# Side work around the first sum of a chunk, in a kernel of four selective-scan layers

## The chip, the cores and the metric

The kernel runs on one core of one Trainium2 chip. The metric is the device time of one execution in microseconds (us); lower is better. TensorE is called PE in the profile (its weight loads PEld), VectorE DVE, ScalarE ACT, GpSimd POOL, and SyncE, which issues the DMAs, SP.

## The reference

Four layers of a vision Mamba block run one after the other over `x` of shape 8 x 48 x 48 x 96, each as `x = x + layer(groupnorm(x))`. A layer projects 96 channels to 2 x 192 (`xz`), puts one half through a depthwise 3x3 convolution and SiLU (`u`), and scans it in four directions: by rows and by columns, forward and backward. Layers 0 to 2 compute this, at each of the 2304 places of a direction, with a state of 16 values per channel:

```python
dA = jnp.exp(dl[..., None] * A)
h = h * dA + (dl * u)[..., None] * Bv[:, :, None, :]
y = jnp.einsum('bkdn,bkn->bkd', h, Cv)
```

`dl` is the softplus of a low-rank projection of `u`; `Bv` and `Cv` are projections of `u`. The four directions are added up with a skip term, normalised over channels, multiplied by `silu(z)` (the other half of `xz`) and projected back to 96 channels. Layer 3 has the same frame with another form of the scan.

## The kernel before

**Tiles and units.** Two images make a pair, four pairs a layer. The 192 channels of a pair lie in three tiles of 128 partitions: 128 channels of either image (t = 0, 1) and the last 64 of both (t = 2). A tile, a phase (ph, rows or columns) and a direction (d) make a group, twelve per pair. The 2304 places of a group are cut into three chunks of 768, and a chunk takes 16 units, one for each n of the 16 states. So a pair has 36 chunks and 576 units. The twelve pairs of layers 0 to 2 have 6912 units; layer 3 ("short") is done in another way, on the places near the ends alone (class `Edge`), and is not touched by the change.

**One unit.** For its n, ACT computes dA (`exp`, L726), TensorE spreads row B over the partitions in PSUM (`spread`, L743), VectorE multiplies it by du = dl * u (L755) and scans (L759), GpSimd multiplies the states by C (L768), and TensorE adds the product to the sum `acc` (`add_up`, L804). In every fourth unit (n % 4 == 3, `pooled`) B comes from a DMA and is multiplied by GpSimd (L698); VectorE then only scans, and dA is put into PSUM instead of B, in `get_ready` of the unit before.

**The sum.** `acc` lies in two banks of PSUM, in a pool with one buffer. `add_up(0)` of a chunk opens it (L798: a matmul of u with the skip weights, or of y so far with the identity), then adds. `add_up(15)` closes it and puts `collect` on the list `late_sums`; `collect` (L819) is ACT's copy of the sum into y. A chunk that is the last of a forward group (`turns`) is not copied: the first chunk of the backward group covers the same places and adds to the same sum, without opening. So a pair has 36 ends of chunks, 30 with a copy and 6 where the sum goes on.

**The order of the work.** `run` writes the order out by hand, unit after unit, and `keep_order` ties every instruction to the one before it on its engine. A unit k issues, in this order: the copy of a sum that the unit before closed (`collected()`, which returns whether there was one: `busy`), what the next units need (`get_ready(k + 1)`: loads three units ahead, the spread of unit k + 1, the decay of unit k + 3), the carries of the scan before (`catch_up`, L650), its own scan, the sum of unit k - 4 (`LAG` = 4), one step of `coming` and one side step. With the lag of four, the last sum of a chunk falls into the unit with n = 3 of the next chunk, and the copy and the next opening into the unit with n = 4. Below these are called unit 3 and unit 4, and so for other n.

**Three kinds of work go on beside.** All are generators of which a step is taken by `next`.
- `coming` is `prepare` of the next chunk: it makes dl and du in two halves (ACT L590 to L601, GpSimd L603 and L604, VectorE L607 to L614), one step per unit from n = 0 on. Between the step of GpSimd and that of L607 stand two bare `yield`s in a row.
- `ahead` is the `prologue` of the next pair: group norm, input projection, convolution (L301, two matmuls of the profile for each of nine taps and five pieces), the x-projection (L454) and its DMAs. `rest` is what is left of the first pair's own prologue.
- `behind` is the `epilogue` of the pair before: for each of 16 pieces of three rows the layer norm, the gate `silu(z)` (L259, with an activation table load ahead of it and one, L260, after it), the product with it (VectorE, L1031) and the output projection, in twelve steps.

`side_step` takes one step of `rest`, or else of `behind` or `ahead`: first the one that holds a PSUM bank (it yielded True), then the one that has made the smaller share of its estimated steps. A prologue whose next tile has no room yet yields `GATED` and gives way. At n = 0 of the last chunk of a pair what is left of both is done at once (`drain`).

Of the kernel before, what the change touches and what calls it, by code (L numbers as in the profile page):

```python
# [53 lines left out]
NS = 16  # L54
# [48 lines left out]
def ss2d_layers_kernel(ctx: ExitStack, tc: tile.TileContext, x_in, consts, weights, out):  # L103
# [449 lines left out]
    def load_dt(c):  # L553
        r = layers[c.l].rank
        c.dts = sm2.tile([64, SCAN], F32, name="dts", tag="dts")
        for b in c.batches:
            q0 = 32 * b if c.t == 2 else 0
            nc.sync.dma_start(
                c.dts[q0 : q0 + r, : c.m],
                state[c.l, c.p]["xd"][c.ph, b, c.d * r : (c.d + 1) * r, c.c0 : c.c0 + c.m],  # L560
            )
# [80 lines left out]
    def collected():  # L642
        some = bool(late_sums)
        while late_sums:
            late_sums.pop(0)()
        return some

    def catch_up():
        while late_act:
            nc.scalar.copy(*late_act.pop(0))  # L650
# [421 lines left out]
    def drain(g):  # L1072
        for _ in g:
            pass

    def step(g):
        next(g, None)
# [7 lines left out]
    def side_step(*sides):  # L1085

        for s in sorted(sides, key=lambda s: (not s.held, s.made / s.total)):
            got = next(s.g, s)
            s.held = got is True
            if got is not s and got is not GATED:  # L1090
                s.made += 1
                return True
        return False
# [3 lines left out]
    def mark():  # L1097
        marks.append(len(tc._region_blocks()[0].instructions))
# [12 lines left out]
    LAG = 4  # L1111
    LOADS, DECAYS = 3, 2

    def run(pairs, short):


        def units():
            for l, p in pairs:
                for gi, (t, ph, d) in enumerate(groups):
                    if l in short:  # L1120
                        c = Edge(l, p, t, ph, d)
                        for i in range(NS // QUAD):
                            yield (l, p, gi * (NS // QUAD) + i), c, i
                        continue
                    group = {}
                    for i in range(len(SCANS)):
                        c = Chunk(l, p, t, ph, d, i, group, c if d == 1 and i == 0 else None)
                        for n in range(NS):
                            yield (l, p, (gi * len(SCANS) + i) * NS + n), c, n

        def begin(l, p, first=False):
            if l not in layers:
                layers[l] = Layer(l)
            return prologue(l, p, l in short, first)

        todo = list(units())

        def get_ready(k):

            def early(ahead, what):  # L1140
                for i in range(0 if k == 0 else k + ahead, min(k + ahead + 1, len(todo))):
                    getattr(todo[i][1], what)(todo[i][2])

            early(LOADS + 1, "load_b")
            early(LOADS, "load")
            if k == 0:
                todo[0][1].decay(todo[0][2])
            if k < len(todo):
                (l, p, _), c, n = todo[k]
                if n == 0 and c.first and l not in short:  # L1150
                    c.group["carry"] = capool.tile([P, NS], F32, name="carry", tag="carry")
                c.spread(n)
            early(DECAYS, "weigh")
            for i in range(k + DECAYS if k else 1, min(k + DECAYS + 1, len(todo))):
                todo[i][1].decay(todo[i][2])

        rest = begin(*pairs[0], first=True)
        while next(rest) is not READY:
            pass
        rest = Side(rest)  # L1160
        chunks = list(dict.fromkeys(c for _, c, _ in todo))
        drain(prepare(chunks[0]))
        behind = ahead = Side()
        coming = iter(())
        done = None
        mark()
        get_ready(0)
        for k, ((l, p, unit), c, n) in enumerate(todo):
            at = pairs.index((l, p))
            following = pairs[at + 1] if at + 1 < len(pairs) else None  # L1170
            if l in short and unit == 0:
                mark()
            per = NS // QUAD if l in short else NS
            all_units = len(groups) * (per if l in short else len(SCANS) * per)
            place["tiles"] = 3 * unit // all_units
            if done:
                behind, done = Side(epilogue(*done), 195), None
            if unit == LAG and following:
                ahead = Side(begin(*following), 300)
            if n == 0:  # L1180
                drain(coming)
                if unit + per == all_units:
                    drain(behind.g)
                    drain(ahead.g)
                coming_to = chunks.index(c) + 1
                coming = prepare(chunks[coming_to]) if coming_to < len(chunks) else iter(())
            if n == max(0, per - 1 - DECAYS):
                drain(coming)
            if n == 10 and coming_to + 1 < len(chunks):
                z = chunks[coming_to + 1]  # L1190
                if (z.l, z.p) == (l, p):
                    load_dt(z)
            busy = collected()
            get_ready(k + 1)
            catch_up()
            c.scan(n)
            if k >= LAG:
                (bl, bp, _), b, bn = todo[k - LAG]
                b.add_up(bn)
                if todo[k - LAG + 1][0][:2] != (bl, bp):  # L1200
                    done = bl, bp
            step(coming)

            for _ in range(10 if l in short else 0 if busy else 1):
                side_step(rest) or side_step(behind, ahead)
        for _, c, n in todo[-LAG:]:
            collected()
            c.add_up(n)
            catch_up()
        collected()  # L1210
        drain(epilogue(*pairs[-1]))

    last = NLAYER - 1
    run([(l, p) for l in range(NLAYER) for p in range(NPAIR)], (last,))

    keep_order(*marks[:2])
# [8 lines left out]
    with tc.If(nc.values_load(again, min_val=0, max_val=1) > 0):  # L1225
        run([(last, p) for p in range(NPAIR)], ())
# [95 lines left out]
```

## Time and profile before

| what | value |
|---|---|
| median of 3 runs | 21,290.81 us (21,287.53 to 21,323.55) |
| the profiled execution, own time | 21,306.41 us |
| its span | 21,304.6 us |
| granted TensorE clock, mean | 0.944 |
| layers 0 to 2: last scan ends at | 19,386 us |
| DVE busy up to there | 17,933.5 us |
| DVE scan with a carry (L759), mean | 1,813 ns |
| DVE multiply (L755), mean | 947 ns |
| POOL product with C (L768), mean | 1,813 ns |
| ACT copy of a sum (L819), 360 times, mean | 1,131 ns |
| PE opening (L798), 4 matmuls of 751 (y) or 582 ns (u), mean | up to 3.0 us |
| PE sum (L804), 27,648 matmuls, four per unit, mean | 519 ns |
| ACT table load (L259, L260), 304 each | 1,283 ns |
| ACT SiLU of the epilogue (L259), mean | 515 ns |
| ACT SiLU over a whole u (L259), 48 times, mean | 2,124 ns |

A line of the timeline reads: start, duration, engine, source line, operation, tile written <- tiles read, form, count, and in brackets the engine's idle time just before it and what ended it. A line of the list of waits reads: engine and line that waited <- engine and line that ended the wait: microseconds in total, times, longest. The view of one source line lists who ended the idle time before its instructions, with microseconds and times.

### The profile page before, as it was taken

To read this page: it belongs to the slowest core of one execution; us is meant where nothing else is said; L and a number is where in the kernel's file an instruction comes from. 1 tells how busy PE (TensorE), PEld (TensorE's weight loads), DVE (VectorE), ACT (ScalarE), POOL (GpSimd) and SP (SyncE) were. 2 spreads that over 40 slices of the span, in tenths; PEclk is the share of its full clock that TensorE was granted. 3 is DMA by queue.
4 is the path that set the end of the run, shared out by engine and by line. 5 is a ranking of instruction groups with operands and counts; after the bars stand their busy time and mean duration, and the time that the engine had idled before them with its cause. 6 is when DMAs were issued, how large, how long until landed. Compare 5 with 4: busy or idle time off the path is not lost. (4 is left out here: it accounts for less than half of the span.)

```text
span 21304.6 us, 229326 instructions
## 1 busy us (share of the span) xinstructions
PE 18651.1 (88%) x64610; PEld 9183.5 (43%) x64610; DVE 18839.5 (88%) x15938; ACT 13518.2 (63%) x23969; POOL 17988.3 (84%) x11081
## 2 busy tenths in 40 slices
PE   8988988998998998998998988988988988988886
PEld 3333443443443443443443443443443443444555
DVE  6999999999999999999999999999999999997453
ACT  5655666666666665665665666665665665666776
POOL 5989898888899899899898889889889888896442
PEclk8999999999999999999999999999999999999887
DMA  4666676676676676676676666666666666664221
GB/s 136 195 190 192 190 196 192 188 192 193 190 198 195 187 200 193 187 202 196 187 200 192 191 193 195 186 194 194 186 195 192 187 194 191 189 193 124 78 72 52
DMA packets 1707633, 3832.97 MB, mean 180 GB/s; under 512 B 238448, under 2 KB 575216, under 8 KB 1693168
## 3 DMA queue, kind: packets, MB, share of 16 engines
q1 hardware_dynamic: 1706352, 3818.21, 61.5%
q8 instruction: 521, 8.54, 0.2%
q14 instruction: 760, 6.23, 0.1%
HBM read 3665.08 MB, written 152.27 MB: 179 GB/s over the span
## 5 line engine op out<-in xcount | busy, mean ns | idle before, releaser
L804 PE MATMUL acc<-cb,cst 128*128 128x384 f32 x27648 | 10772.4, 519 | 0.0
L768 POOL TENSOR_TENSOR cb<-cb,da 128x768 f32<-128x768 f32 x5184 | 9350.0, 1813 | 1586.3 <-DVE da L759 953.8
L804 PEld LDWEIGHTS acc<-cb,cst 128*128 128x128 f32 x27648 | 5031.9, 197 | 3972.4 <-issue 1530.2
L759 DVE TENSOR_TENSOR_SCAN da<-da,carry,b 128x768 f32<-128x768 f32 x3456 | 6267.3, 1813 | 219.0 <-DVE b L755 1.4
L755 DVE TENSOR_TENSOR b<-du,b 128x768 f32<-128x768 f32 x5184 | 4910.0, 947 | 789.6 <-PE b L743 780.1
L726 ACT ACTIVATE da<-dl,a 128x768 f32<-128x768 f32 x5184 | 4770.6, 926 | 94.0 <-POOL cb L768 61.2
L743 PE MATMUL b<-brow,pick 48*128 48x512 bf16 (+3 forms) x10368 | 2660.3, 338 | 1516.2 <-DVE da L759 1184.7
L726 ACT ACTIVATE b<-dl,a 128x768 f32<-128x768 f32 x1728 | 1560.5, 903 | 2927.1 <-DVE da L759 2673.6
L768 POOL TENSOR_TENSOR cb<-cb,bb 128x768 f32<-128x768 f32 x1728 | 3133.2, 1813 | 188.1 <-issue 63.6
L698 POOL TENSOR_TENSOR bb<-bb,du 128x768 f32<-128x768 f32 x1728 | 3131.4, 1812 | 124.5 <-DMA bb<-xd 78.8
L759 DVE TENSOR_TENSOR_SCAN da<-da,b 128x768 f32<-128x768 f32 x1728 | 3029.5, 1753 | 107.4 <-DVE b L755 0.9
L743 PEld LDWEIGHTS <-pick 48*128 48x128 bf16 (+1 forms) x10368 | 667.2, 97 | 4345.3 <-DVE da L759 2285.7
L759 DVE TENSOR_TENSOR_SCAN bb<-b,carry,bb 128x768 f32<-128x768 f32 x1152 | 2069.7, 1797 | 9.1 <-ACT b L726 6.1
L301 PE MATMUL ps<-pad,diag 128*128 128x480 f32 (+1 forms) x4320 | 1995.8, 560 | 17.0 <-DVE du L611 11.5
L650 ACT COPY carry<-da 128x1 f32<-128x1 f32 x3456 | 626.9, 181 | 1068.6 <-DVE da L759 1055.7
L590 ACT ACTIVATE ps<-ps,w 128x384 f32<-128x384 f32 (+1 forms) x912 | 496.6, 545 | 1115.0 <-PE ps L585 1114.4
L301 PEld LDWEIGHTS ps<-pad,diag 128*128 128x128 f32 x4320 | 807.4, 192 | 721.1 <-issue 293.4
L603 POOL TENSOR_TENSOR lg<-lg,w 128x384 f32<-128x384 f32 (+1 forms) x912 | 891.5, 977 | 196.7 <-ACT w L601 196.6
L759 DVE TENSOR_TENSOR_SCAN bb<-b,bb 128x768 f32<-128x768 f32 x576 | 999.2, 1735 | 15.5 <-ACT b L726 11.9
L585 PE MATMUL ps<-dts,w 6*128 6x384 f32 (+5 forms) x2432 | 819.7, 522 | 182.0 <-DVE du L611 65.9
L604 POOL TENSOR_TENSOR lg<-lg,e 128x384 f32<-128x384 f32 (+1 forms) x912 | 889.3, 975 | 71.2
L798 PE MATMUL acc<-y,cst 128*128 128x384 f32 x1008 | 625.3, 751 | 275.2 <-ACT y L819 176.2
(141 smaller groups left out, 17322.1 us busy)
## 6 DMA issues: line engine op xcount, KB each, us to landing
cb<-xd SPq DMA_DIRECT2D x4736, 384.0 KB
cb<-xd SPq DMA_DIRECT2D x4736, 192.0 KB
bb<-xd SPq DMA_DIRECT2D x1152, 384.0 KB
bb<-xd SPq DMA_DIRECT2D x1152, 192.0 KB
yd<-y SPq DMA_DIRECT2D x48, 1152.0 KB
ey<-yd SPq DMA_DIRECT2D x256, 216.0 KB
brow<-xb SPq DMA_DIRECT2D x576, 72.0 KB
ex<-xs SPq DMA_DIRECT2D x256, 108.0 KB
```

Source lines behind the costliest of these rows:

```text
L301: nc.tensor.matmul(ps[:, :m], ly.diag[:, int(t == 2), j, :], pad[:, r0 + dy : r0 + dy + nr, dx : dx + W], start=(j == 0), stop=(j == 8),)
L585: nc.tensor.matmul(o[:, :m], ly.dtw[q0 : q0 + r, k, chans], dts[q0 : q0 + r, at], start=True, stop=True,)
L603: nc.gpsimd.tensor_sub(lg, lg, w1)
L604: nc.gpsimd.tensor_add(lg, lg, e)
L650: nc.scalar.copy(*late_act.pop(0))
L698: nc.gpsimd.tensor_mul(b, b, self.du)
L726: nc.scalar.activation(da, self.dl, AF.Exp, scale=columns_of(self.l, self.t, self.ph, self.d, n))
L743: nc.tensor.matmul(b[:, z : z + zm], w, self.brow[:k, z : z + zm], start=True, stop=True)
L755: nc.vector.tensor_mul(b, self.du, b)
L759: nc.vector.tensor_tensor_scan(way(h), way(da), way(b), start, ALU.mult, ALU.add)
L768: nc.gpsimd.tensor_mul(c, c, h)
L804: nc.tensor.matmul(self.acc[:, a, : self.m // 2], ident, c[:, a, :], start=False, stop=(n == NS - 1 and not self.turns),)
```

## The change

The step of `coming` and the side steps become a function, `beside`. In a unit in which a sum was copied (`busy`, unit 4) it is called ahead of `add_up`, with one side step where there was none; in every other unit it stays behind `add_up`. The unit whose `add_up` is the last of a chunk (`ends`, unit 3) has no side step any more, also where the sum goes on and nothing is copied; there, unit 4 keeps the side step that it had. So a pair has 540 side steps where it had 546. Layer 3 stays as it was.

```diff
             get_ready(k + 1)
             catch_up()
             c.scan(n)
+
+
+            def beside():
+                step(coming)
+
+                for _ in range(10 if l in short else 0 if ends else 1):
+                    side_step(rest) or side_step(behind, ahead)
+
+            ends = l not in short and k >= LAG and todo[k - LAG][2] == NS - 1
+            if busy and l not in short:
+                beside()
             if k >= LAG:
                 (bl, bp, _), b, bn = todo[k - LAG]
                 b.add_up(bn)
                 if todo[k - LAG + 1][0][:2] != (bl, bp):
                     done = bl, bp
-            step(coming)
-
-            for _ in range(10 if l in short else 0 if busy else 1):
-                side_step(rest) or side_step(behind, ahead)
+            if not (busy and l not in short):
+                beside()
```

## The prediction

> **What bounds the kernel now.** First the busy line, then one engine's idle time, then who ended it. The busy line of the page:
>
> ```profile
> PE 18651.1 (88%) x64610; PEld 9183.5 (43%) x64610; DVE 18839.5 (88%) x15938; ACT 13518.2 (63%) x23969; POOL 17988.3 (84%) x11081
> ```
>
> Three engines stand near 88%, so the average names no bound. By stretches, layers 0 to 2 end at 19,386 us, and there DVE is busy 17,933.5 us: it sets the pace, one scan of some 1.75 us per unit and a multiply of 0.95 us in three of four. Its idle time there is 1,453 us, and only that can be won. The list of waits and, second, the view of line 1031 up to 19,400 us, say what most of it waits for:
>
> ```profile
> DVE b L755 <- PE b L743: 780.1, 644, 4.8
> ...
> PEld acc L798 <- ACT y L819: 304.0, 187, 5.4
> ...
> PE acc L798 <- ACT y L819: 231.8, 149, 5.0
> ...
> ACT y L819 <- PE acc L804: 160.3, 172, 2.0
> ```
>
> ```profile
>   ACT ps L259: 73.5, 41
> ```
>
> L755 waits for its spread B (L743), TensorE waits at the opening sum (L798) for ACT's copy of the old one (L819), and the copy waits for the last sum in only 172 of 360 cases: in the others ACT itself came late. Counting L759's scans in program order (6912, 16 per chunk) gives every instruction its unit. The idle time then gathers: 410 us lie before the multiply of unit 6 at 359 chunk boundaries with a copy, 1,142 ns each (zero in the 72 boundaries whose sums go on), and 73 us before L1031, behind the scan of unit 3. One boundary in the timeline:
>
> ```profile
> 5267.11 1.73 DVE L759 TENSOR_TENSOR_SCAN bb<-b,bb 128x768 f32<-128x768 f32 x1
> ...
> 5267.68 1.56 PE L804 MATMUL acc<-cb,cst 128*128 128x384 f32 x4
> 5268.05 1.28 ACT L259 ACT_TABLE_LOAD   x1
> ...
> 5269.34 0.52 ACT L259 ACTIVATE ps<-ps 128x432 f32<-128x432 f32 x1
> 5269.87 1.28 ACT L260 ACT_TABLE_LOAD   x1
> 5269.89 0.60 DVE L1031 TENSOR_TENSOR eyc<-eyc,ps 128x432 f32<-128x432 f32 x1 [1.05 <-ACT ps L259]
> ...
> 5272.09 0.79 ACT L819 COPY y<-acc 128x768 f32<-128x768 f32 x1
> ...
> 5272.93 2.85 PE L798 MATMUL acc<-y,cst 128*128 128x384 f32 x4 [3.27 <-ACT y L819]
> ...
> 5277.94 0.96 DVE L755 TENSOR_TENSOR b<-du,b 128x768 f32<-128x768 f32 x1 [1.68 <-PE b L743]
> ```
>
> The last sum of the old chunk ends at 5269.2, but ACT is in a gated SiLU of the epilogue issued as side work of unit 2 (3.1 us with its two table loads); the copy starts 2.9 us late, TensorE stands 3.27 us, and the spread of unit 6, behind opening and first sum in TensorE's queue, is 1.68 us late for DVE. L1031, side work of unit 3, makes DVE wait for the same SiLU.
>
> **What the Trainium skill says.** "PSUM — Partial Sum Buffer", section "Engine vs sequencer instructions": the queues of ScalarE, VectorE and GpSimdE are strictly first in, first out, and matmuls start and end in program order. The trace agrees: no matmul passes the waiting L798. The same page, section "PSUM bank collisions raise a hardware error", wants accesses to a bank kept apart by semaphores; the trace has TensorE idle 535.8 us at L798 until L819 is done. "ScalarE: Activation LUTs", section "What ACT_TABLE_LOAD costs", states 1283 ns for the load and about 1380 ns of drain. The trace has the 1283 ns, but next to no gap: 5268.05 + 1.28 is 5269.33, and the activation starts at 5269.34. I take 1.28 + 0.52 + 1.28 = 3.08 us per SiLU.
>
> **The change, part by part.** The opening sum stands in unit 4 of a chunk, the last sum of the one before in unit 3.
>
> 1. *step(coming) ahead of the opening sum: 0.* In unit 4 it is the fifth step of prepare, which lies between two bare yields and issues nothing.
>
> 2. *The side step of unit 3 moves to unit 4, ahead of the opening sum.* On TensorE the order was last sum, side, spread 5, opening; it becomes last sum, spread 5, side, opening: the same sum of times before the opening, no gain. On ACT the step's work no longer stands ahead of the copy. It was there in 72 boundaries; taking it out of the traced order (the copy then starts at the later of the last sum's end and the ACT work before the side step) brings the copies forward by 37 us in all. Not all of it reaches DVE: 210 of 359 boundaries have a late unit 6. I take half: -18 us.
>
> 3. *What falls into units 1 and 2 shifts.* Where sums go on (72 boundaries) the side step of unit 3 is dropped, none is given back; all later side work of the pair slips by one step each time, six per pair. I walked the yields of prologue and epilogue through the loop's rules, before and after; for before, this puts a convolution into unit 3 111 times, as the trace has it. The sides come in a rhythm that met the boundaries badly: the epilogue's SiLU (192 in these layers) is the side step of unit 2 at 39 of the 359 boundaries, and of 13 with the new rule. At the 39, unit 6's wait is 2,514 ns, at the other 320, 975 ns: 26 x 1.54 = 40 us. The SiLU in unit 1 rises from 22 to 25, Ln and Exp (L1006) there from 8 to 14; such boundaries lie about 0.55 us above others of their kind: +5 us. Together -35 us.
>
> 4. *L1031 leaves unit 3.* DVE's wait for the SiLU, 73 us, ends there in every case, as nothing is issued in unit 3; the multiply then stands behind the scan of unit 4. In the 13 that keep their SiLU in unit 2, the copy is as late as before, and what is won at L1031 is lost in unit 6. The other 26 of 39 win: -49 us.
>
> 5. *Matmuls ahead of the opening.* The steps that now fall there hold 0.91 us of TensorE work per boundary, those of unit 3 held 0.77 (from rows such as L301's 576 ns, two per step): 0.14 x 359 = 51 us. TensorE idles before the opening at 263 of 359 (1,089 ns on average), which hides some of it; without that cover all 51 us would be exposed. A gain is excluded, as it is only more work on the same queue. I take 20.
>
> 6. *DMAs, POOL, DVE.* The step's DMAs pass the loads of unit 8 on SP's queue. Loads go out three units ahead (over 8 us), so 0. One is special: at a pair's start the epilogue's first load waits for the store of y (ey issued at 5014.66, 3.34 us after ex). It is now queued a unit earlier, and the loads for unit 9 wait behind it: at 11 changes of pair, 0 to 2 us each; the cover is three units; I take 0 and keep 22 as the end. POOL's side work (pad memsets, L434) slips by a unit; with 20 us at most in either direction, since POOL was idle over 3,300 us, I take 0. Slots: 540 per pair for some 495 to 520 steps; none is left for the drains, so 0.
>
> Sum: -18 - 35 - 49 + 20 = -82 us, that is about -80. The profiled execution took 21,306.4 us (span 21,304.6), so 21,226; it lies 16 us above the median of the three runs, and against that I say 21,211.
>
> **The rivals.**
> - *Nothing to be measured (0.22).* Other long ACT steps (the SiLU over a whole u, 4.7 us, comes into unit 2 at 6 boundaries) take the SiLU's place, and half of parts 3 and 4 is lost: -18 - 42 + 40 = -20, or 21,271. For: both are averages over few boundaries. Against: ACT side work ahead of the copy falls from 1.23 to 0.88 us per boundary in units 1 to 3.
> - *The copy was most of it (0.15).* The copy starts 748 ns after the last sum on average, 269 us in all. If the lighter units 1 to 3 end half of that, and the 73 us at L1031 go wholly: 135 + 73 - 20 (part 5) = 188: 21,103. Against: exps of L726 and prepare's steps lie in the same queue.
> - *Slower: side matmuls expose the opening (0.08).* Where the copy is done before TensorE has gone through the moved step, every matmul of it delays opening, first sum and spread 6, then DVE. It decides once the opening's idle time is used up: unit 6 is already late in 210 cases. Were all 51 us of part 5 exposed, the 22 of part 6 come in, and parts 3 and 4 only changed places with new bad meetings, -18 + 51 + 22 = +55: 21,346.
> - *That the change does not act* is excluded: the order on TensorE's queue is written out and kept.
>
> **How the numbers follow.** Forecast 0.55: 21,211, between 21,160 (part 5 hidden, part 2 whole) and 21,255 (part 5 exposed, the re-meeting half as good). The range takes in most of the larger gain and of the rival of no change: 21,100 to 21,290; what is left out is the slower case and the tails, under 0.2. About 0.2% (43 us) is what a measurement of this kernel can tell: faster means under 21,248. Nearly all of the forecast and all of the larger gain: 0.70; same 0.22; slower 0.08.
>
> **What would show it.** Right: L1031's wait for L259 before 19,400 us falls from 73.5 to almost nothing; L798's idle time until L819 falls from 535.8 to some 400; L755's for L743 from 780 to some 700; DVE's idle time in layers 0 to 2 loses 80 of 1,453 us, its busy time nothing. Wrong: L798 waits for something other than L819 or ACT's carries (the moved step waits itself), L1031's wait reappears in another unit, or the multiplies of units 8 and 9 take up what unit 6 gives back.

## The result and the profile after

| | before | changed |
|---|---|---|
| median of 4 runs | 21,290.11 us | 21,138.65 us |
| lowest to highest | 21,287.53 to 21,323.55 us | 21,131.57 to 21,152.58 us |
| ratio, 95% interval | | 0.9929 (0.9917 to 0.994) |
| profiled span | 21,304.6 us | 21,129.7 us |
| granted TensorE clock, mean | 0.944 | 0.951 |

The change gains 151 us, 0.71%, where 80 us had been forecast: the direction and the places were right, the size was nearly double. The busy line of the page after:

```profile
PE 18566.6 (88%) x64610; PEld 9118.1 (43%) x64610; DVE 18834.4 (89%) x15938; ACT 13520.6 (64%) x23969; POOL 17984.5 (85%) x11081
```

The instruction counts are those of before, and up to the last scan DVE is busy as long (17,933.5 us before, 17,926.9 now): only its idle time can have gone. TensorE is busy 85 us less with the same matmuls (18,651.1 before), and its granted clock is higher; what that has to do with the change is taken up with the second experiment. The lines of the list of waits that answer to those of before:

```profile
DVE b L755 <- PE b L743: 678.8, 619, 6.2
...
PEld acc L798 <- ACT y L819: 241.7, 248, 4.1
...
ACT y L819 <- PE acc L804: 177.4, 177, 4.1
...
PE acc L798 <- ACT y L819: 142.6, 139, 3.7
```

DVE waits 101 us less for its spread. The two lines of L798 behind L819 are the weight loads and the matmuls of the same openings, so most of one wait stands in both. Their sum, 535.8 us before and 384.3 now, which the prediction took for TensorE's idle time, counts it about twice. The matmul line alone falls by 89 us (231.8 to 142.6). Counted once per opening, whatever ended the wait, TensorE's idle time there falls from 391 to 258 us. The view of L1031 up to the last scan has nothing under "its engine sat idle before it" any more, where it had 73.5 us behind L259.

Counted by unit as in the prediction, the balance of layers 0 to 2 is: DVE's idle time from 1,452.5 to 1,294.1 us (-158), the last scan from 19,386.2 to 19,221.2 us. Of the 158, the multiply of unit 6 gives 105 (412.8 to 307.4), L1031 gives 74, L611 13; L607, the step of prepare that waits for GpSimd, takes 32 back.

### The profile page after: what moved, and what is told of

It is laid out like the page before. It is cut to its first block, busy times and chain, and to the rows that moved or that the text cites. A ratio compares the mean times of both kernels' runs of the same rounds, so it can differ in the third digit from the quotient of the medians.

```text
span 21129.7 us, 229163 instructions
## 1 busy us (share of the span) xinstructions
PE 18566.6 (88%) x64610; PEld 9118.1 (43%) x64610; DVE 18834.4 (89%) x15938; ACT 13520.6 (64%) x23969; POOL 17984.5 (85%) x11081
## 5 line engine op out<-in xcount | busy, mean ns | idle before, releaser
L755 DVE TENSOR_TENSOR b<-du,b 128x768 f32<-128x768 f32 x5184 | 4912.0, 948 | 685.4 <-PE b L743 678.8
L698 POOL TENSOR_TENSOR bb<-bb,du 128x768 f32<-128x768 f32 x1728 | 3131.3, 1812 | 183.4 <-DMA bb<-xd 142.8
L650 ACT COPY carry<-da 128x1 f32<-128x1 f32 x3456 | 627.1, 181 | 1086.3 <-DVE da L759 1076.4
L798 PE MATMUL acc<-y,cst 128*128 128x384 f32 x1008 | 619.1, 745 | 192.2 <-ACT y L819 127.2
```

What stands on the lines that cost most here:

```text
L698: nc.gpsimd.tensor_mul(b, b, self.du)
L755: nc.vector.tensor_mul(b, self.du, b)
```

## The experiments

All times are medians; the difference is against runs of the kernel before on the same chip, taken between them. The changed kernel stands at -151 us.

| run | us | against before | ratio, 95% interval |
|---|---|---|---|
| e1_move_only | 21,241.45 | -52 | 0.9973 (0.9963 to 0.9984) |
| e2_rhythm_only | 21,242.25 | -51 | 0.9976 (0.9966 to 0.9987) |
| e3_step_behind_sum | 21,361.29 | +68 | 1.0034 (1.0022 to 1.0046) |
| e4_spread_ahead | 21,088.52 | -205 | 0.9902 (0.9887 to 0.9917) |
| e8_before_no_silu | 21,107.37 | -185 | 0.9911 (0.9897 to 0.9924) |
| e5_after_no_silu | 21,175.85 | -117 | 0.9942 (0.9929 to 0.9956) |
| e6_both | 21,239.19 | -53 | 0.9974 (0.9965 to 0.9984) |
| e7_both_lighter | 20,910.43 | -382 | 0.9822 (0.9808 to 0.9835) |
| e9_spread_lighter | 20,926.78 | -362 | 0.9824 (0.981 to 0.9837) |
| e10_lighter_only | 21,169.55 | -119 | 0.9938 (0.9924 to 0.9951) |

**The move without the rhythm (e1_move_only).** To the changed kernel:

```diff
             ends = l not in short and k >= LAG and todo[k - LAG][2] == NS - 1
+            ends = busy and unit == LAG or ends and not todo[k - LAG][1].turns
```

> The side step moves from unit 3 to unit 4, ahead of the opening sum, but every step keeps its place in the rhythm: where the sum goes on, unit 3 keeps its step, and the epilogue starts in unit 5 as before, so the SiLU stays in unit 2 at 39 boundaries. By the prediction's terms (-18 for the copy, +20 for the matmuls, L1031's 73 us lost again in unit 6) it should stand within 20 us of the kernel before. The rival, that the move itself is most of the gain and was sized too small, expects -80 to -110 us. In both, L1031 waits for L259 no more.

It gains 52 us, which lies in neither of the expected ranges. Because every step keeps its place in the sequence, each boundary can be compared with itself, over the ten units from the scan of unit 1 to that of unit 10. At the 39 with the SiLU in unit 2, L1031's wait ends (73.5 to 0.4 us in the view of the line) and the wait of unit 6 grows from 2,514 to 3,854 ns; the ten units are 31 ns shorter. So what is won at L1031 is lost in unit 6, as forecast. At the 71 other boundaries whose moved step has ACT work, the copy starts 0.55 us nearer to the last sum, 39 us in all, and the ten units shrink by 680 ns (57 without matmuls) and 1,590 ns (14 with matmuls): 61 us in all. So more reaches DVE than the copies were moved by; the next experiment shows a reason. At the 189 where the step is matmuls alone it is 24 ns, 4.5 us in all: TensorE's order there is worth nothing, as forecast. The rest gives 17 us. (These sums come from the two profiled executions, whose spans differ by 81 us where the medians differ by 52; the shares are what counts.)

**The rhythm without the move (e2_rhythm_only).** To the kernel before:

```diff
-            for _ in range(10 if l in short else 0 if busy else 1):
+            ends = l not in short and k >= LAG and todo[k - LAG][2] == NS - 1
+            none = busy and unit != LAG or ends and todo[k - LAG][1].turns
+            for _ in range(10 if l in short else 0 if none else 1):
```

> The kernel before, with its side step still in unit 3 and none in unit 4, but with the rhythm of the changed kernel: no side step in unit 3 where the sum goes on, and the epilogue's first step in unit 4 of a pair. The SiLU then stands in unit 2 at 13 boundaries and not 39. The prediction's terms give -35 for the wait of unit 6 and -49 for L1031: about -84 us against before. The rival, that the move is most of it, expects -40 to -60 us here. L1031's wait for L259 should fall to a third, some 25 us.

It gains 51 us, not 84, as the rival said, and L1031's wait falls to 18.7 us. Move and rhythm alone give 52 + 51 = 103 us, together 151: there are some 48 us that neither has. The size is rough: each of the three figures has an interval of some 20 to 25 us either way, and the profiled spans give 20 us. The place is clear: at 16 boundaries the rhythm now puts a SiLU on the moved step itself. Against before, the ten units of these 16 lose 6 us by the move alone, gain 14 by the rhythm alone and gain 85 by both; at the other boundaries both together give 46 us less than their sum. Without the move this SiLU stands in unit 3, right ahead of the copy; the timeline of one of the 16, rhythm only:

```profile
7100.23 1.56 PE L804 MATMUL acc<-cb,cst 128*128 128x384 f32 x4
...
7102.53 1.28 ACT L259 ACT_TABLE_LOAD   x1
...
7103.83 0.52 ACT L259 ACTIVATE ps<-ps 128x432 f32<-128x432 f32 x1
...
7104.36 1.28 ACT L260 ACT_TABLE_LOAD   x1
...
7105.65 1.48 ACT L819 COPY y<-acc 128x768 f32<-128x768 f32 x1
...
7107.19 2.92 PE L798 MATMUL acc<-u,skip 128*128 128x384 f32 x4 [4.97 <-ACT carry L650]
...
7113.43 0.96 DVE L755 TENSOR_TENSOR b<-du,b 128x768 f32<-128x768 f32 x1 [5.71 <-PE b L743]
```

The same boundary in the changed kernel:

```profile
7081.78 1.56 PE L804 MATMUL acc<-cb,cst 128*128 128x384 f32 x4
...
7084.09 1.47 ACT L819 COPY y<-acc 128x768 f32<-128x768 f32 x1
...
7085.59 1.28 ACT L259 ACT_TABLE_LOAD   x1
...
7085.61 1.56 PE L798 MATMUL acc<-u,skip 128*128 128x384 f32 x4 [1.84 <-ACT carry L650]
...
7086.89 0.52 ACT L259 ACTIVATE ps<-ps 128x432 f32<-128x432 f32 x1
...
7087.42 1.28 ACT L260 ACT_TABLE_LOAD   x1
7088.22 0.54 DVE L607 SCALAR_TENSOR_TENSOR ps<-ps,lg 128x384 f32<-128x384 f32 x1
...
7088.39 0.50 PE L743 MATMUL b<-brow,pick 48*128 48x512 bf16 x2
...
7089.18 0.95 DVE L755 TENSOR_TENSOR b<-du,b 128x768 f32<-128x768 f32 x1
```

The SiLU's three ACT pieces are the same 3.1 us in both; ahead of the copy DVE waits 5.71 us at the multiply of unit 6, behind it not at all: the last line has no bracket. (The bracket of L798 names L650, a carry that ACT ran right behind the copy.)

The 5.71 us are more than the SiLU's 3.1. From the end of the last sum to the opening it is 5.40 us with the rhythm alone and 2.27 us in the changed kernel, which is the SiLU. From the opening to the multiply of unit 6 it is 6.24 and 3.57 us, though the same matmuls stand there (the opening takes 2.92 and 1.56 us). Below are these two stretches, first with the rhythm alone and then in the changed kernel; PEclk is the granted clock of TensorE as a share of full speed:

```profile
core 0: us, PE busy (x) PEld busy (x) DVE busy (x) ACT busy (x) POOL busy (x), PEclk, DMA share, GB/s
7107.19:7113.43 6.24, 6.24 (x11) 2.74 (x12) 0.53 (x3) 3.78 (x7) 3.61 (x3) 0.52 0.76 252
```

```profile
7085.61:7089.18 3.57, 3.57 (x11) 1.85 (x12) 3.47 (x4) 3.53 (x4) 3.49 (x4) 1.00 0.88 310
```

So about 3.1 us of the loss are the later copy, and about 2.7 us are the same matmuls taking longer at about half the clock. It is not this boundary alone. The clock records of these traces have two values, full and half. In the kernel before, the clock was half for some time between the opening and the multiply of unit 6 at 142 of the 359 boundaries, and 338 of the 410 us of unit 6's wait lie at these; in the changed kernel it was so at 74 boundaries, with 186 of 305 us. In the trace of before, half clock goes with a long idle time of TensorE just before the opening: it is there at 12 of 198 boundaries with less than 1 us, at 74 of 103 with 1 to 2 us, and at 56 of 58 with more. At the 71 boundaries of the first experiment the move takes the number of those with half clock from 39 to 18, which fits the 61 us won for 39 us of earlier copies. This suggests that the higher mean clock of the changed kernel comes, at least in part, from the shorter waits at the openings, and in turn shortens what follows them. No run sets the clock, so neither this nor the share of the whole gain that passes through it is shown.

Once more the table loads show no drain beside them, which "ScalarE: Activation LUTs" of the Trainium skill has in its section "What ACT_TABLE_LOAD costs": 7102.53 + 1.28 is 7103.81, and the SiLU starts at 7103.83. Over the 16 boundaries the wait of unit 6 is 79.5 us in this run and 8.1 us in the changed kernel, and their ten units 31.93 and 27.50 us: 16 x 4.43 = 71 us.

**The side step of unit 4 behind the sum (e3_step_behind_sum).** To the changed kernel:

```diff
-            if busy and l not in short:
-                beside()
             if k >= LAG:
...
-            if not (busy and l not in short):
-                beside()
+            beside()
```

> The changed kernel with the side step of unit 4 behind the opening and first sum, and none in unit 3. If the place ahead of the opening matters because the step's matmuls (0.91 us per boundary) use the time in which TensorE waits for the copy, they now stand between first sum and spread 6, and about 0.3 to 0.7 us comes back at the boundaries where unit 6 is late: +60 to +140 us against the changed kernel, so near -50 against before. If only ACT's order matters, it stays within 20 us of the changed kernel, at -150. In both, the start of the copy stays as in the changed kernel.

It is 219 us slower than the changed kernel and slower than before. Here the view of L798, the engine's idle time before it (again with loads and matmuls added up):

```profile
  ACT y L819: 634.5, 510
```

The copy starts 471 ns after the last sum on average (463 in the changed kernel), so ACT is not it. But TensorE now stands idle for the copy (1,199 ns per opening, 719 in the changed kernel) and runs the side step's matmuls later, between first sum and spread 6: the wait of unit 6 rises from 307 to 460 us. The boundaries with half clock between the opening and that multiply rise from 74 to 118. The direction was the first theory's, the size beyond its range (60 to 140 us).

**The spread of unit 6 ahead of the opening (e4_spread_ahead).** To the changed kernel:

```diff
-                c.spread(n)
+                if n not in c.b or c.pooled(n):
+                    c.spread(n)
...
             if busy and l not in short:
                 beside()
+                if l < NLAYER - 1:
+                    c.spread(n + 2)
```

> The changed kernel with the spread of unit 6 issued in unit 4 ahead of the opening, in layers 0 to 2. If the wait at unit 6 (305 us of DVE's idle time in the changed kernel) is only the spread's place behind opening and first sum, it goes; TensorE's queue is 0.5 us longer ahead of the opening and must first wait for the scan of unit 4, so the later units 8 and 9 take some of it back: -100 to -250 us against the changed kernel, -250 to -400 against before. The rival, that TensorE's backlog of opening and sums only moves on to the spread of unit 8, expects within 40 us of the changed kernel, with L755's wait in unit 8 or 9 grown by as much as unit 6 loses.

It beats the changed kernel by 54 us, which lies between the two expectations (100 us or more; 40 at most). The wait of unit 6 goes, from 307 to 3 us; that of unit 8 grows from 105 to 348. So most of it only moved on, which is the rival's mechanism, to the next spread behind the same matmuls: TensorE has a backlog.

**No SiLU near the copy (e8_before_no_silu, e5_after_no_silu).** A flag is up while a side's next step is a SiLU or the scaling of x (layer 3 is left as it is):

```diff
+            late = n in (1, 2, 3) and (place["long"] or place["gate"])
-            for _ in range(10 if l in short else 0 if busy else 1):
+            for _ in range(10 if l in short else 0 if busy or late else 1):
```

in the kernel before, and with `n in (1, 2)` in `beside` of the changed kernel.

> The kernel before, in which no side step is taken in units 1, 2 and 3 while the next one of a side would be a SiLU (or the group norm's scaling of x): such steps wait for unit 5 or later. Nothing else moves. If ACT work ahead of the copy is the cause, the wait at L1031 (73 us) goes and the wait of unit 6 falls from 412 to 300 us or less, and it gains 100 to 150 us against before, as much as the whole change, without any step moved ahead of the opening. The rival, that the place of the step ahead of the opening is what gains, expects no more than the 50 us of the rhythm alone.

> The changed kernel, with no side step in units 1 and 2 while the next one would be a SiLU or the scaling of x. By a walk through the rules 38 SiLUs of the epilogue and 7 over a whole u leave these units. If ACT's queue ahead of the copy is what is left to gain, -30 to -70 us against the changed kernel (-180 to -220 against before), the start of the copy is nearer to the last sum. If what is left at unit 6 is TensorE's own chain of opening and first sum, within 20 us of the changed kernel.

The first gains 185 us, more than the 100 to 150 expected and more than the whole change, and no side step in it is moved from unit 3 to unit 4: the wait of unit 6 falls from 413 to 254 us, L1031's from 74 to 7, and the boundaries with half clock behind the opening from 142 to 76. It is thus shown that taking ACT's long steps away from the copy is alone worth as much as the change. The second misses both expectations: the wait of unit 6 falls from 307 to 208 us, as the first theory wanted, but those of units 0, 1 and 8 rise by 81 us together and L607's by 17, and the run ends 35 us behind the changed kernel, with intervals that overlap. Postponed SiLUs gather in units 0 and 4 (28 and 32 by a walk through the rules, 12 and 16 before; the traces show the 32 and 16 of unit 4); that these cause the new waits is argued, not shown.

**Both, and a lighter backlog (e6_both, e7_both_lighter, e9_spread_lighter, e10_lighter_only).** e6 joins e4 and e5. The other three have, besides:

```diff
-                for _ in range(10 if l in short else 0 if ends else 1):
+                for _ in range(10 if l in short else 0 if ends or n in (5, 6) else 2 if n in (12, 13) else 1):
```

e7 has it (with `late`) on top of e6, e9 on top of e4, e10 on the changed kernel.

> The run before this one together with the spread of unit 6 ahead of the opening. If the two gains are of different waits they add up: -250 to -280 us against before. If the earlier copy only helps the opening, which no longer holds up unit 6, the sum is smaller: near the -205 of the spread ahead alone.

> As the run before, and no side step in units 5 and 6 of any chunk, but two each in units 12 and 13. With the spread of unit 6 ahead, the wait moved to unit 8 (348 us), because TensorE still has opening, sums and side work to catch up with. If that backlog is the bound, taking some 1.7 us of side work out of it halves the wait of unit 8: -100 to -170 us against the run before. The rival, that units 12 and 13 then fall behind in the same way (two matmuls of a side step more each), expects within 30 us of it.

> The changed kernel with the spread of unit 6 ahead of the opening, no side step in units 5 and 6 and two each in units 12 and 13; SiLUs go where the rhythm puts them. If keeping SiLUs out of units 1 and 2 costs as much as it gains (as +37 us against the changed kernel says), this is as good as the run with that rule or better: -380 to -430 us against before. If with the spread ahead the copy's lateness weighs more, it is worse than that run, at -300 to -370.

> The changed kernel with no side step in units 5 and 6 and two each in units 12 and 13, and the spread of unit 6 in its old place. If TensorE's backlog alone is the bound, most of the gain comes without the spread ahead: -300 us or more against before. If the spread's place behind the opening holds unit 6 up whatever follows, only the waits of units 8 and 9 (171 us) can shrink, and it stays within 100 us of the changed kernel: -150 to -250 against before.

e6 loses 152 us against e4, where a gain or no difference had been expected: the wait of unit 8 is 412 us there, L607's 195. e7 takes it down to 128 us and gains 329 us over e6, about twice the most that was expected; DVE's idle time falls to 1,064 us. Units 12 and 13 show no wait of L755 and only 29 us more idle time of DVE than in e6 (136 and 107), so the extra steps cost little there: with prepare's own work on DVE these two units last 3.2 and 3.3 us in the kernel before, where most others last 2.7 to 3.0 (1.75 where VectorE only scans). The list of waits of e7, where the line of the multiply is 759 and of the spread 747:

```profile
DVE b L759 <- PE b L747: 357.8, 442, 5.8
```

That is half of the changed kernel's 678.8. e9 falls into its second range, but only 20 us behind e7, which the intervals do not tell from nothing: the rule for SiLUs is worth little by then. e10 falls into neither of its ranges and shows that the lighter backlog alone brings no gain (-119 against -151, with intervals that overlap): the wait of unit 6 stays at 318 us, that of unit 9 rises to 125. Spread ahead (-205) and lighter units (-119) together give -362: only together do they gain much. Both e7 and e9 clearly beat the changed kernel.

## Why the prediction was right, and where a size failed

1. *step(coming): 0.* Not tested by itself; the trace gives no cause to doubt it.

2. *The copy freed of the moved step: -18 us.* The mechanism is right, the size failed, and this is the term to mend. The prediction had 72 boundaries with ACT work in the step, their copies 37 us earlier in all, and let half reach DVE. e1 shows 61 us at 71 such boundaries, where the copies came 39 us earlier: not half of it arrives but more than all. The half was a guess from the share of all boundaries at which unit 6 was late. Boundaries with ACT work ahead of the copy are late more often (51 of these 71, against 122 of the 249 that have neither such work nor a SiLU in unit 2). And the prediction counted a later copy as a shift alone and put nothing for the matmuls behind it, which the trace shows at half clock at 39 of the 71 before and at 18 with the move. And the term was made with the old rhythm: with the new one, 16 SiLUs fall into the moved step. Changed kernel against rhythm only, the 80 boundaries with ACT work in the step and no SiLU in unit 2 give 123 us over their ten units.

3. *The rhythm: -35 us, with L1031 -49 us.* Together 84 us forecast, 51 measured in e2. The walk was right that there are 26 fewer boundaries with a SiLU in unit 2, but the sum did not price where the steps land: 14 of the 39 now have a SiLU in the moved step, and as long as that stands ahead of the copy it costs nearly as much (at the 16 such boundaries the ten units take 31.9 us with the rhythm alone, 32.8 before, 27.5 with both). Parts 2 and 3 were added up as if independent; the difference between 103 and 151 lies here. That the sum came out on the right side owes something to luck: against the runs, part 2 was 43 us too small, parts 3 and 4 were 33 us too large, and the interplay was left out.

4. *L1031: 73 us end, 24 of them lost again in unit 6.* Right in kind: at the 13 boundaries that have the SiLU in unit 2 now (only 5 of them had it before), unit 6 waits 3,731 ns in the changed kernel, where the 39 of before had 2,514: 16 us lost again.

5. *More matmuls ahead of the opening: +20 us.* Not seen as a loss at the boundaries whose step is matmuls alone (-24 ns each in e1); e1 doesn't change how many matmuls there are, so the 51 us of the heavier steps weren't measured by themselves.

6. *DMAs, POOL, DVE: 0.* No new wait of DVE of that kind over 32 us appears; L607's 32 us, a wait for GpSimd, is there in e2 too (33 us), so it belongs to the rhythm. GpSimd itself waits 64 us more for the loads of B at L698 (78.8 to 142.8), also with the rhythm alone (140.9), but DVE waits for L698 only 11.3 us.

Of the rivals, the one with the larger gain, that the lateness of the copy was most of it, came nearer than its 0.15 said: the measured -151 is nearer to its -188 than to the forecast's -80. It was held down because exps and prepare's steps share ACT's queue; they do, and the copy is still 463 ns late, from 748, which is 38% of the lateness ended where the rival had half. The slower rival did not show: its mechanism is side matmuls ahead of the opening that delay it, and e3, which takes them away from there, is slower, not faster. The named signs came: L798's two lines behind L819 at 384.3 us (some 400 foretold), L755's wait at 678.8 (some 700), L1031's gone; and units 8 and 9 did not take up what unit 6 gave back (106 and 67 us before, 105 and 66 now). DVE's idle time fell by twice what was named, and that alone told that a size was wrong.

## What to carry to other kernels

When an engine evacuates a buffer that another waits for, price everything that its queue holds ahead of the copy, by the boundary and not by the average: the boundaries that have such work are late more often. Then read the granted clock behind the wait: here the matmuls that follow a long idle time of TensorE often ran at half clock, and at the boundary shown a copy 3.1 us later cost 5.71 us. If an edit shifts a sequence of side steps, list where each long step lands after it, and cost the landing together with the other parts of the edit. A spread that must overtake an opening needs the queue behind it to be lightened as well, or the wait moves to the next one.

## What was not expected

- Filling TensorE's wait for the copy is worth more than the whole change: with the same steps in the same units, the place behind or ahead of the sum is worth 219 us over 359 boundaries, 0.6 us each, of 0.9 us of matmuls.
- Two edits that gain little or lose when alone (a spread ahead, 54 us; lighter units, 32 us behind) gain 211 us together.
- What makes e6 slower than e4 by 152 us stays open: the waits of units 8 and L607 are longer, and the granted clock is the lowest of all runs, 0.942 against 0.946, with half clock for 1,918 and 1,737 us up to the last scan; no run tells cause and effect apart.
